# A decoder layer on one core: bfloat16 conversions moved to GpSimd, and the cross attention's output normalization moved from ScalarE into the weights and the residual

## The chip, the cores and the metric

The kernel runs on one core of a Trainium2 chip. The metric is the device time of one execution in microseconds (us). Three runs of the kernel before took 2183.72, 2186.22 and 2188.77 us, so the median is 2186.22 us.

The engines are named as in the profile: PE is TensorE (matrix products and transposes), DVE is VectorE, ACT is ScalarE, POOL is GpSimd, SP is SyncE, which here only issues DMAs. PEld is the loading of weights into TensorE.

## The reference, cut to what matters

The layer takes 32 sequences of 256 tokens with 256 features. It has three parts, each with a residual and a layer norm without gain behind it:

```
x = layernorm(x + self_attention(x))            # 16 heads of 64, 4 key heads, rotary, alibi
x = layernorm(x + cross_attention(x, ctx))      # 16 heads of 16, windows of 64, a mask
x = layernorm(x + ffn(x))                       # 8-bit quantized inputs, ternary weights
```

Two places matter. The cross attention ends in a projection of a normalized row o, with a gain g, a shift b, weights W and a bias:

```
m   = mean(o);  var = mean((o - m)**2)
out = ((o - m) * rsqrt(var + eps) * g + b) @ W.T + bias
```

The feed-forward part quantizes the inputs of its products, once before the gate and up products (256 features) and once before the down product (1024 features):

```
scale = 127 / max(abs(x));  xq = round(x * scale) / scale
```

## The kernel before, in words

All 32 sequences are worked through one after the other, with neighbours overlapped: the self attention of a sequence runs beside the cross attention of the one before and the feed-forward part of the one before that. A sequence has 16 slots (four units m of four parts each). The loop at the end of `tile_decoder_kernel` walks over the slots and emits, by hand, what PE, DVE and ACT do, in that order. Stages that do not belong to the attention's inner units are generators (`self_output`, `cross_inputs`, `cross_output`, `feed_forward`, `prepare_cross`); `yield n` means that the generator goes on n slots later. `last` is a list of operations that `flush()` emits at the end of a part, so an operation put there lands behind the exponentials of that part on ACT.

`tc.manual_schedule` covers PE, DVE and ACT, whose instructions stand in the order of emission. The order on POOL and on SP is set by the framework's planner from what it expects to be ready; in the trace, for example, L186 of the context's normalization runs behind L584, and L184 and L185 run ahead of it. Each engine works through its own queue in order and waits at semaphores for the others.

The lines that the change and the prediction touch:

- `prepare_cross` (from L208) runs once at the start. It multiplies the weights of the four cross projections by the gain of their layer norm (POOL, L224), and the shift through the weights gives a bias (PE, L245; DVE, L252).
- `stats` (L177, L178) computes mean and variance of a row on DVE. `rstd_of` (L184 to L186) makes the factor 1/sqrt(var + eps) and the shift -mean * factor on POOL, in three small instructions. `scaled` (L198) applies both on ACT. `transposed` (L204, L205) transposes a tile on PE and copies it out of PSUM on ACT.
- `cross_output` (from L762) is called for the two halves t of a sequence. It normalizes the row `on` with `stats`, `rstd_of` and `scaled`, transposes it into `zoT`, multiplies it with the weights `xo_w` (PE, L775), adds the residual x1 (DVE, L779), and normalizes the result, x2.
- `feed_forward` (from L786) finds the largest absolute value of x2 on DVE, scales and rounds on POOL by adding MAGIC = 12582912 (L803, output `tr`, in the code xi), takes MAGIC away again with an output in bfloat16 on DVE (L805, `xib`), and lets SP issue transposing DMAs into `xiT` (L809). PE multiplies it with the gate and up weights (L816), ACT takes the tanh (L830), DVE the products (L831, L837). The hidden row `gu` is then treated in the same way: the maximum (L843), four small DVE instructions (L845 to L850), POOL (L852), DVE (L855, `hib`), SP (L857, `hiT`), and the down product on PE (L863).
- Beside them on POOL: the rotary additions (L354, L584 to L586), the copy `R` of the reciprocals of the softmax sums (L455), the mask (L612, L615), and the factors of the other layer norms. `R` waits for a transposing DMA (`planes`) of what DVE spread out in `wide` (L443).
- The attention's own chain: scores on PE (`s`, L393), the maximum and the bias on DVE (`p`, `nm`, L409), exponentials on ACT (L427), transposes on PE (`t`, L471), the copy `pT` on ACT (L480), the products with the values on PE (`o`, L492). The cross attention has the same chain: `xs` (L674), L688, L704, `xt` (L713), the copy `xpT` (L715), `xo` (L729). The context is normalized in `cross_inputs` (`cs` by L198) and transposed into `zcT`. `self_output` makes the normalized row `row` on DVE (L538), transposed into `zqT`, and the query projection `xq` (L550).

Of the kernel before, what the change touches and what calls it, by code (L numbers as in the profile page):

```python
# [10 lines left out]
BF16 = mybir.dt.bfloat16  # L11
# [3 lines left out]
ALU = mybir.AluOpType  # L15
# [36 lines left out]
def kernel(  # L52
# [50 lines left out]
    def work(name, shape, bufs=2, dtype=F32):  # L103
        return sb.tile(list(shape), dtype, tag=name, name=name, bufs=bufs)
# [103 lines left out]
    def prepare_cross():  # L208


        nc.sync.dma_start(vecs_sb, vecs)
        nc.sync.dma_start(cols_sb, cols)
        for j, (w, dst) in enumerate(
            (
                (wxk, xkv_w[:, :, 0:D]),
                (wxv, xkv_w[:, :, D : 2 * D]),
                (wxq, xq_w),
                (wxo, xo_w),
            )
        ):  # L220
            raw = work("tr", [P, NDC, D], 3)
            nc.sync.dma_start(raw, w.rearrange("(c p) n -> p c n", p=P))
            for dc in range(NDC):
                nc.gpsimd.tensor_scalar(  # L224
                    dst[:, dc, :], raw[:, dc, :], vecs_sb[:, j, 0, dc : dc + 1], None, ALU.mult
                )
            if j == 0:
                nc.sync.dma_start(wo_sb, Wo.rearrange("(c p) n -> p c n", p=P))
            if j in xbias:
                more = work("xp", [P, 512])  # L230
                row = more[:, 0:D]
                nc.sync.dma_start(row, rows[j].partition_broadcast(P))
                for dc in range(NDC):
                    nc.gpsimd.tensor_scalar(
                        more[:, D + dc * P : D + (dc + 1) * P],
                        ones,
                        vecs_sb[:, j, 1, dc : dc + 1],
                        None,
                        ALU.mult,
                    )  # L240
            yield 2
            pb = bank("mm")
            if j in xbias:
                for dc in range(NDC):
                    nc.tensor.matmul(  # L245
                        pb[:, 0:D],
                        more[:, D + dc * P : D + (dc + 1) * P],
                        raw[:, dc, :],
                        start=(dc == 0),
                        stop=(dc == NDC - 1),  # L250
                    )
                nc.vector.tensor_tensor(xbias[j], pb[:, 0:D], row, ALU.add)  # L252
            else:
                for ch in range(NDC):
                    for dc in range(NDC):
                        nc.tensor.matmul(
                            pb[:, ch : ch + 1],
                            raw[:, dc, ch * P : (ch + 1) * P],
                            vecs_sb[:, j, 1, dc : dc + 1],
                            start=(dc == 0),  # L260
                            stop=(dc == NDC - 1),
                        )
                nc.vector.tensor_tensor(xbcol[j], pb[:, 0:NDC], cols_sb[:, j, :], ALU.add)
            yield 2
# [497 lines left out]
    def cross_output(b, t):  # L762
        s = state[b]
        on = s["on", t]
        mv = stats(on, "zo")
        rstd = rstd_of(mv, "zo")
        yield
        last.append(partial(scaled, on, on, rstd))
        yield 2
        zoT = work("zT", [P, NDC, P])  # L770
        transposed(zoT, on, "zoT")
        yield 2
        py = bank("xw")
        for dc in range(NDC):
            nc.tensor.matmul(py[:, 0:D], zoT[:, dc, :], xo_w[:, dc, :], start=(dc == 0), stop=(dc == NDC - 1))  # L775
        if t == 0:
            s["x2"] = work("x2", [P, NT, D])
        h = s["x2"][:, t, :]
        nc.vector.tensor_tensor(h, py[:, 0:D], s["x1", t], ALU.add)  # L779
        mv = stats(h, "x2")  # L780
        rstd = rstd_of(mv, "x2")
        yield
        last.append(partial(scaled, h, h, rstd))


    def feed_forward(b):  # L786
        x2 = state[b]["x2"]

        s = small("ffs", NT)
        nc.vector.tensor_reduce(s, x2, AX.X, ALU.max, apply_absolute_value=True)  # L790
        nc.vector.tensor_scalar(s, s, QUANT_MIN, None, ALU.max)
        up = small("ffup", NT)
        nc.vector.reciprocal(up, s)
        nc.vector.tensor_scalar(up, up, 127.0, None, ALU.mult)
        g_of = small("ffg", NT)
        nc.vector.tensor_scalar(g_of, s, ff_scale["gate"], 0.5, ALU.mult, ALU.mult)
        u_of = small("ffu", NT)
        nc.vector.tensor_scalar(u_of, s, ff_scale["up"], None, ALU.mult)
        nc.vector.tensor_tensor(u_of, u_of, g_of, ALU.mult)
        xi = work("tr", [P, NT, D], 3)  # L800
        xib = work("xib", [P, NT, D], 1, BF16)
        for t in range(NT):
            nc.gpsimd.tensor_scalar(xi[:, t, :], x2[:, t, :], up[:, t : t + 1], MAGIC, ALU.mult, ALU.add)  # L803
        yield
        nc.vector.tensor_scalar(xib, xi, MAGIC, None, ALU.subtract)  # L805

        xiT = work("xiT", [P, NT, NDC, P], 1, BF16)
        for t in range(NT):
            nc.sync.dma_start_transpose(xiT[:, t, :, :], xib[:, t, :])  # L809
        yield 3  # L810
        gu = work("gu", [P, NT, INNER], 1)

        def hidden(name, t, half):
            pg = bank("ff")
            for dc in range(NDC):
                nc.tensor.matmul(  # L816
                    pg,
                    xiT[:, t, dc, :],
                    ff_w[name][:, dc, half * 512 : (half + 1) * 512],
                    start=(dc == 0),  # L820
                    stop=(dc == NDC - 1),
                )
            return pg


        for t in range(NT):
            for half in range(2):
                pg = hidden("gate", t, half)
                cols = gu[:, t, half * 512 : (half + 1) * 512]
                nc.scalar.activation(cols, pg, AF.Tanh, scale=g_of[:, t : t + 1])  # L830
                nc.vector.scalar_tensor_tensor(cols, cols, 1.0, pg, ALU.add, ALU.mult)  # L831
            yield 1 if t == 0 else 3
        for t in range(NT):
            for half in range(2):
                pg = hidden("up", t, half)
                cols = gu[:, t, half * 512 : (half + 1) * 512]
                nc.vector.tensor_tensor(cols, cols, pg, ALU.mult)  # L837
            yield 1 + t
        d_ofs, hiTs = [], []
        for t in range(NT):  # L840

            m = small("ffm", 1)
            nc.vector.tensor_reduce(m, gu[:, t, :], AX.X, ALU.max, apply_absolute_value=True)  # L843
            sh = small("ffsh", 1)
            nc.vector.tensor_scalar(sh, m, u_of[:, t : t + 1], QUANT_MIN, ALU.mult, ALU.max)  # L845
            hup = small("ffhup", 1)
            nc.vector.reciprocal(hup, sh)
            nc.vector.tensor_scalar(hup, hup, u_of[:, t : t + 1], 127.0, ALU.mult, ALU.mult)
            d_of = small("ffd", 1)
            nc.vector.tensor_scalar(d_of, sh, ff_scale["down"], None, ALU.mult)  # L850
            d_ofs.append(d_of)
            nc.gpsimd.tensor_scalar(gu[:, t, :], gu[:, t, :], hup, MAGIC, ALU.mult, ALU.add)  # L852
            yield
            hib = work("hib", [P, INNER], 2, BF16)
            nc.vector.tensor_scalar(hib, gu[:, t, :], MAGIC, None, ALU.subtract)  # L855
            hiT = work("hiT", [P, NIC, P], 2, BF16)
            nc.sync.dma_start_transpose(hiT, hib)  # L857
            hiTs.append(hiT)
        yield 2
        for t in range(NT):  # L860
            py = bank("ffo")
            for ic in range(NIC):
                nc.tensor.matmul(  # L863
                    py[:, 0:D], hiTs[t][:, ic, :], ff_w["down"][:, ic, :], start=(ic == 0), stop=(ic == NIC - 1)
                )
            y = x2[:, t, :]
            nc.vector.scalar_tensor_tensor(y, py[:, 0:D], d_ofs[t], y, ALU.mult, ALU.add)
            mv = stats(y, "y")
            rstd = rstd_of(mv, "y")
            yield  # L870
            last.append(partial(scaled, y, y, rstd))
        last.append(partial(nc.sync.dma_start, out[b].rearrange("(t p) d -> p t d", p=P), x2))
        del state[b]
# [179 lines left out]
```

## Time and profile before

| what | value |
|---|---|
| runs, median of three | 2186.22 us (2183.72 to 2188.77) |
| profiled execution, span from first to last instruction | 2184.1 us; no other time of that execution is recorded |
| PE busy | 2096.9 us, 96% |
| DVE busy | 1778.0 us, 81% |
| ACT busy | 1600.0 us, 73% |
| POOL busy | 1285.1 us, 59% |
| mean clock granted to TensorE | 0.983 |
| one 64.65 us stretch from 1015.00 us on: PE, DVE, ACT, POOL busy | 64.21, 55.40, 49.91, 39.88 us |
| HBM traffic | 39.50 MB read, 8.39 MB written |

The profile is one execution on the chip. A row of the groups gives line, engine and operation, output and inputs by name, shapes and count; then the busy time in us and the mean duration in ns; then the idle time of that engine just ahead of these instructions and whose end released them. A row of the waits gives who waited for whom, with the total in us, how often, and the longest. The chain follows the work that ended last back from the end, and gives for each piece its start and its length. Matrix products are pipelined and their ends are modelled, so PE may stand still for some tenths of a microsecond while it counts as busy; such a stall shows when a block of products takes longer than the same block elsewhere. A line can be that of a helper, so L198 or L204 stands for several callers, which the names of the tiles tell apart.

### The profile page before, as it was taken

The page shows a single profiled execution, that of the slowest core. Times are in us where ns is not written, and L with a number is a line of the kernel's source. Part 1 is how long each engine was busy: PE and PEld are TensorE (multiplying, and loading weights), DVE is VectorE, ACT ScalarE, POOL GpSimd, SP SyncE. Part 2 cuts the span into 40 slices and gives each one's busy share as a digit, 9 for nine tenths or more (in the row PEclk, how much of TensorE's full clock was granted, in tenths as well). Part 3 has the DMA queues.
Part 4 walks back from the last instruction along what each step waited for, and adds up shares of the span by engine and source line. Part 5 has one row for each costly group of instructions (what it writes and reads, how often), then busy time and mean ns, then how long its engine had stood idle before and what let it go on. Part 6 is the DMA issues. An engine that isn't in the chain of part 4 may idle for free.

```text
span 2184.1 us, 54367 instructions
## 1 busy us (share of the span) xinstructions
PE 2096.9 (96%) x17316; PEld 1606.7 (74%) x17316; DVE 1778.0 (81%) x6949; ACT 1600.0 (73%) x4833; POOL 1285.1 (59%) x1977
## 2 busy tenths in 40 slices
PE   7899999999999999999999999999999999999983
PEld 5677777777777777777777777777777777777751
DVE  4777888888888888888888888888888888888765
ACT  2478778777778877777877777877777877777862
POOL 4555665566655656655656655656666566666542
PEclk9899999999999999999999999999999999999986
DMA  7432333333333334334334333333343333333211
GB/s 219 111 75 72 82 75 83 77 79 86 89 72 78 83 71 91 86 71 86 76 76 89 82 77 79 78 81 83 86 82 76 81 82 74 90 81 69 53 42 32
DMA packets 326589, 177.57 MB, mean 81 GB/s; under 512 B 242976, under 2 KB 296096, under 8 KB 326304
## 3 DMA queue, kind: packets, MB, share of 16 engines
q1 hardware_dynamic: 324608, 170.52, 34.6%
q8 instruction: 139, 2.28, 0.5%
q10 hardware_dynamic: 1696, 3.57, 0.5%
q14 instruction: 146, 1.20, 0.2%
HBM read 39.50 MB, written 8.39 MB: 22 GB/s over the span
## 4 chain that ended last, share of the span: by engine, by line
PE 74%; DVE 11%; ACT 5%; POOL 4%; DMA 4%; issue 1%; SPq 0%; ACTq 0%; POOLq 0%; DVEq 0%
PE wo L513 10%; PE o L492 8%; PE proj L330 8%; PE t L471 8%; PE s L393 8%; PE ff L816 5%; PE xt L713 4%; PE xo L729 3%; PE xq L550 3%; PE xs L674 3%; PE ffo L863 3%; PE xk L622 3%; DVE p L409 2%; PE xw L775 2%; PE v L362 2%; DVE xib L805 2%
## 5 line engine op out<-in xcount | busy, mean ns | idle before, releaser
L427 ACT ACTIVATE p<-p,nm 128x256 f32<-128x256 f32 x1024 | 511.6, 512 | 197.7 <-DVE nm L409 197.7
L409 DVE CUSTOM_DVE_ANT_0 p<-s,alibi 128x256 f32<-128x256 f32 x1024 | 364.6, 416 | 6.3 <-PE s L393 6.3
L480 ACT COPY pT<-t 128x512 f32<-128x512 f32 x512 | 276.1, 601 | 89.6 <-PE t L471 89.3
L704 ACT ACTIVATE xp<-xp,xnm 128x128 f32<-128x128 f32 x1024 | 331.8, 416 | 0.0
L688 DVE CUSTOM_DVE_ANT_0 xp<-xs,mask 128x128 f32<-128x128 f32 x1024 | 225.9, 285 | 68.1 <-PE xs L674 68.1
L455 POOL COPY R<-planes 128x1024 uint16<-128x1024 uint16 x128 | 175.4, 1370 | 176.3 <-DMA planes<-wide 164.6
L471 PE MATMUL t<-ident,p 128*128 128x128 f32 x2048 | 266.4, 273 | 0.9 <-ACT p L427 0.9
L492 PE MATMUL o<-pT,v 128*64 128x256 f32 x2048 | 260.8, 386 | 1.3 <-ACT pT L480 1.1
L393 PE MATMUL s<-kT,qT 64*128 64x256 f32 x2048 | 255.7, 389 | 0.0
L513 PE MATMUL wo<-wo_sb,oT 128*128 128x256 f32 x1024 | 248.0, 386 | 0.4 <-ACT xpT L715 0.3
L354 POOL TENSOR_TENSOR qT<-qT,other 128x512 f32<-128x512 f32 x128 | 169.4, 1323 | 127.6 <-DMA other<-psin 66.4
L330 PE MATMUL proj<-xT,wq_sb 128*128 128x256 f32 x1024 | 243.1, 381 | 0.0
L471 PEld LDWEIGHTS t<-ident,p 128*128 128x128 f32 x2048 | 234.2, 141 | 9.4 <-ACT p L427 2.6
L393 PEld LDWEIGHTS s<-kT,qT 64*128 64x128 f32 x2048 | 187.3, 186 | 63.4 <-issue 14.3
L492 PEld LDWEIGHTS o<-pT,v 128*64 128x64 f32 x2048 | 143.9, 136 | 104.4 <-issue 21.2
L513 PEld LDWEIGHTS wo<-wo_sb,oT 128*128 128x128 f32 x1024 | 194.9, 193 | 30.9 <-ACT xpT L715 1.1
L427 ACT ACTIVATION_READ_ACCUMULATOR p<-p,nm 128x1 f32 x1024 | 208.0, 203 | 0.0
L330 PEld LDWEIGHTS proj<-xT,wq_sb 128*128 128x128 f32 x1024 | 185.8, 191 | 21.1 <-issue 0.4
L831 DVE SCALAR_TENSOR_TENSOR gu<-gu,ff 128x512 f32<-128x512 f32 x128 | 82.6, 684 | 84.5 <-ACT gu L830 84.3
L713 PEld LDWEIGHTS xt<-ident,xp 128*128 128x128 f32 x1024 | 110.6, 141 | 53.7 <-issue 38.5
L713 PE MATMUL xt<-ident,xp 128*128 128x128 f32 x1024 | 143.3, 281 | 2.1 <-ACT xp L704 2.0
L339 DVE TENSOR_TENSOR psin<-proj,rs_sb 128x512 f32<-128x512 f32 x160 | 109.8, 686 | 38.2 <-PE proj L330 34.6
(146 smaller groups left out, 4325.7 us busy)
## 6 DMA issues: line engine op xcount, KB each, us to landing
other<-psin SPq DMA_DIRECT2D x640, 64.0 KB, 2.0
xT<-in_xt_dram SPq DMA_DIRECT2D x32, 256.0 KB, 2.8
xs<-in_x_dram SPq DMA_DIRECT2D x32, 256.0 KB, 2.8
cs<-in_ctx_dram SPq DMA_DIRECT2D x32, 256.0 KB, 2.8
other<-qb SPq DMA_DIRECT2D x64, 128.0 KB, 2.1
kTz<-tr SPq DMA_DIRECT2D x256, 32.0 KB, 2.0
other<-qb SPq DMA_DIRECT2D x128, 64.0 KB, 2.0
out_dram<-x SPq DMA_DIRECT2D x32, 256.0 KB, 2.3
```

The lines of the kernel that those rows point to most:

```text
L330: nc.tensor.matmul(pq[:, c * L : (c + 1) * L], w[:, dc, c * P : (c + 1) * P], xT[:, dc, :], start=(dc == 0), stop=(dc == NDC - 1),)
L393: nc.tensor.matmul(banks[half][:, rr * L : (rr + 1) * L], qT[rows_, rr, qc * P : (qc + 1) * P], kT[rows_, kc, :], start=(rr == 0), stop=(r ...
L409: nc.vector.tensor_tensor_reduce(p[:, cols], banks[half][:, cols], alibi[:, 2 * (4 * kc + 2 * rp + rr) + half, :], -0.125, 3.0e38, ALU.add ...
L427: nc.scalar.activation(p[:, cols], p[:, cols], AF.Exp, bias=nm[:, rr : rr + 1], scale=-1.0, accum_out=s["sums", i // 2][:, e : e + 1],)
L455: nc.gpsimd.tensor_copy(R.bitcast(U16).rearrange("p (n z) -> p z n", z=2), s.pop(("planes", m)).rearrange("p z r q -> p z (r q)"),)
L471: nc.tensor.transpose(pt[:, j * P : (j + 1) * P], p[half][:, rr * L + kk * P : rr * L + (kk + 1) * P], ident,)
L480: nc.scalar.copy(pT, pt)
L492: nc.tensor.matmul(po[half * HD : (half + 1) * HD, rp * L : (rp + 1) * L], s["v"][:, kk, (2 * kc + half) * HD : (2 * kc + half + 1) * HD], ...
L513: nc.tensor.matmul(py[:, 0:D], s["oT", qc, kc][:, r, :], wo_sb[:, 4 * kc + r, :], start=(kc == 0 and r == 0), stop=(kc == 1 and r == 3),)
L688: nc.vector.tensor_tensor_reduce(p[:, cols], banks[2 * half + j // 2][:, j % 2 * P : (j % 2 + 1) * P], s["mask"][:, qc, :], -1.0, 3.0e38, ...
L704: nc.scalar.activation(p[:, cols], p[:, cols], AF.Exp, bias=s["xnm", i][half][:, j : j + 1], scale=-1.0)
L713: nc.tensor.transpose(pt[:, j * P : (j + 1) * P], p[:, j * P : (j + 1) * P], ident)
```

## The change

There are three edits. First, `prepare_cross` centres the weights of the cross output once: a product with ones gives the sum over the input features, and 1/D of it is subtracted from each row of weights. A row multiplied by such weights loses its mean by itself. Second, `cross_output` no longer normalizes `on` in front of the transpose: `rstd_of`'s third instruction and the ACT operation are gone, the transpose takes `on` as it is, in the same slot as before, and the factor is applied to the projection in the instruction that adds the residual. Third, the two conversions to bfloat16, `xib` and `hib`, are done by POOL in place of DVE, straight behind the POOL instructions that make their inputs and one yield earlier in the order of emission; `xib` in two instructions, one for each half.

```diff
@@ prepare_cross
                 nc.vector.tensor_tensor(xbias[j], pb[:, 0:D], row, ALU.add)
+                if j == O_:
+                    for dc in range(NDC):
+                        nc.tensor.matmul(pb[:, D:], ones, dst[:, dc, :], start=(dc == 0), stop=(dc == NDC - 1))
+                    for dc in range(NDC):
+                        nc.vector.scalar_tensor_tensor(
+                            dst[:, dc, :], pb[:, D:], -1.0 / D, dst[:, dc, :], ALU.mult, ALU.add
+                        )
@@ cross_output
         mv = stats(on, "zo")
-        rstd = rstd_of(mv, "zo")
-        yield
-        last.append(partial(scaled, on, on, rstd))
-        yield 2
+        rstd = small("rstd_zo", 1)
+        nc.gpsimd.tensor_scalar(rstd, mv[:, 1:2], EPS, None, ALU.add)
+        nc.gpsimd.tensor_tensor(rstd, rstd, neg_half[:, 0:1], ALU.pow)
+        yield 3
         zoT = work("zT", [P, NDC, P])
...
-        nc.vector.tensor_tensor(h, py[:, 0:D], s["x1", t], ALU.add)
+        nc.vector.scalar_tensor_tensor(h, py[:, 0:D], rstd, s["x1", t], ALU.mult, ALU.add)
@@ feed_forward
             nc.gpsimd.tensor_scalar(xi[:, t, :], x2[:, t, :], up[:, t : t + 1], MAGIC, ALU.mult, ALU.add)
+        for t in range(NT):
+            nc.gpsimd.tensor_scalar(xib[:, t, :], xi[:, t, :], MAGIC, None, ALU.subtract)
         yield
-        nc.vector.tensor_scalar(xib, xi, MAGIC, None, ALU.subtract)
...
             nc.gpsimd.tensor_scalar(gu[:, t, :], gu[:, t, :], hup, MAGIC, ALU.mult, ALU.add)
+            hib = work("hib", [P, INNER], 2, BF16)
+            nc.gpsimd.tensor_scalar(hib, gu[:, t, :], MAGIC, None, ALU.subtract)
             yield
-            hib = work("hib", [P, INNER], 2, BF16)
-            nc.vector.tensor_scalar(hib, gu[:, t, :], MAGIC, None, ALU.subtract)
             hiT = work("hiT", [P, NIC, P], 2, BF16)
             nc.sync.dma_start_transpose(hiT, hib)
```

## The prediction

> **What bounds the kernel now.** I read four views of the profile, in this order: the busy shares, the waits, the chain that ended last, and the groups of instructions. The shares say that TensorE (PE) is the engine to look at:
>
> ```profile
> PE 2096.9 (96%) x17316; PEld 1606.7 (74%) x17316; DVE 1778.0 (81%) x6949; ACT 1600.0 (73%) x4833; POOL 1285.1 (59%) x1977
> ```
>
> One sequence repeats every 64.65 us (a 64.65 us stretch from 1015 us on has PE busy for 64.21 us at a granted clock of 1.00). So a gain can only come from PE's few stalls, and from the two ends of the span. The waits name those stalls; the columns are total us, times, longest:
>
> ```profile
> PE xo L729 <- ACT xpT L715: 12.0, 30, 0.7
> ...
> PEld o L492 <- ACT pT L480: 8.2, 33, 1.5
> ...
> PE zqT L204 <- DVE row L538: 6.7, 10, 1.7
> ```
>
> The first two come about once for each of the 32 sequences; the third is irregular. The chain around the first (start us, length us, what) shows its origin:
>
> ```profile
> 1041.62 1.46 DVE xib L805
> ...
> 1046.53 0.59 ACT x L539
> 1047.11 0.98 ACT p L427 x4
> 1048.10 0.96 ACT xpT L715 x2
> 1049.06 0.04 issue
> 1049.10 0.43 PE xo L729 x16
> ...
> 1056.46 2.33 PE o L492 x16
> ```
>
> VectorE's bfloat16 conversion xib sits ahead of the softmax pieces p. They come late, ScalarE's exponentials start late, and from 1044.05 to 1063 us ScalarE has no idle time in its timeline. PE pays twice. First at xo: from the start of xs (1047.54) to the start of xq (1049.46) are 1.92 us, against 0.62 + 0.59 = 1.21 us for the same two blocks at 1029.71 and 1062.98: 0.71 us. Then at o, 2.33 us against 1.88 us at 1021.15: 0.45 us. Together 1.16 us in each sequence.
>
> Why does xib take 1.46 us? The groups:
>
> ```profile
> L855 DVE TENSOR_SCALAR hib<-gu 128x1024 bf16<-128x1024 f32 x64 | 58.1, 908 | 8.9 <-POOL gu L852 8.9
> L805 DVE TENSOR_SCALAR xib<-tr 128x512 bf16<-128x512 f32 x32 | 44.3, 1384 | 8.3 <-POOL tr L803 7.5
> L852 POOL TENSOR_SCALAR gu<-gu,ffhup 128x1024 f32<-128x1024 f32 x64 | 71.7, 1120 | 79.2 <-DVE ffhup L848 79.0
> L803 POOL TENSOR_SCALAR tr<-x,ffup 128x256 f32<-128x256 f32 x64 | 29.9, 480 | 0.0
> ```
>
> The fastest xib took 426 ns, the median 1482 ns. At 1041.54 to 1042.81 POOL runs L585, and xib, issued at 1041.60, ends 0.28 us after it. This DVE form stands still while POOL works.
>
> **The change part by part.**
>
> *xib leaves DVE.* 1.48 us go from the stretch in front of p. On DVE: the statistics of on, then p from about 1042.2 instead of 1043.56; the scores exist by then (PE issued that unit's half from 1040.76 to 1041.7). ScalarE starts at about 1042.7 instead of 1044.05. Its order then is four exponentials (1.97 us), two scalings (1.0), two exponentials (1.0), the two copies xpT (0.95): done at 1047.6, and PE wants them at 1048.16. The stall of 0.71 goes, with some 0.5 us to spare. What is late next is L538, a conversion-free DVE TENSOR_SCALAR that can be held up by POOL too (409 ns usual, 1259 ns when it fell on L586); even held until 1045.0 it leaves these copies in time.
>
> *on's scaling leaves ScalarE.* 64 ACTIVATE of 599 ns, some 0.5 us of it in each place because neighbours overlap. One lies at 1050.20, between the two stalls. PE comes to o 0.71 us earlier, so o's second copy has to be earlier by more than that. The activation gu L830 after it needs PE's gate product, which bounds its start to about 1050.3 instead of 1051.46; the copy ends 1.16 us earlier, at 1056.05, where PE would want it at 1055.95. I take 0.34 of the 0.45 us. Sum of both stalls: 0.71 + 0.34 = 1.05 us a sequence, 29 times: **-30.5 us**.
>
> *The factor at the residual.* L779 becomes a scalar_tensor_tensor; L867 is that form (476 against 422 ns): 64 x 0.054 = 3.5 us of DVE, hidden as DVE idles 45.2 us ahead of L779 for PE. Its new wait on POOL's rstd costs nothing: at 1045.55 the factor is there, L779 runs at 1060.71. Were POOL 15 us late, the p pieces behind L779 would wait, and ScalarE for them. POOL loses L186, 64 x 265 ns = 17 us.
>
> *The centring*, once: four matmul records (0.86 us after the 0.43 us records of L245) and two DVE instructions of about 0.48 us in front of the first scores at 35.3 us, where PE waits for DVE and ScalarE afterwards. Nothing at best (2.6 us of waiting at 58.5 us can hide it), 1.8 us at worst; I take +0.9.
>
> *hib and xib on POOL.* No row shows POOL subtracting one constant with a bfloat16 output. Lower end: the two-operation multiply and add at 1120 ns for 1024 columns and 480 for 256, so 0.83 ns a column and 0.27 fixed. Upper end: L612, a compare and a multiply, 721 ns for 128 columns, so 3.5 ns a column and 3.9 us for a hib. Between them lie the only one-operation rows:
>
> ```profile
> L224 POOL TENSOR_SCALAR xkv_w<-tr,vecs_sb 128x256 f32<-128x256 f32 x4 | 3.7, 932 | 12.0 <-DMA tr<-in_wxk_dram 11.6 <-DMA tr<-in_wxv_dram 0.3
> L234 POOL TENSOR_SCALAR xp<-ones,vecs_sb 128x128 f32<-128x128 f32 x4 | 2.4, 604 | 0.0
> ```
>
> Their medians are 924 and 602 ns: (0.924 - 0.602) / 128 = 2.52 ns a column, 0.28 fixed. They have the second operation left out, as the new instructions have, so I take them: **hib 2.86 us, xib 2 x 0.92 us**. POOL grows by 64 x 2.86 + 64 x 0.92 - 17 = 225 us, from 59 to 69%.
>
> The Trainium skill speaks both ways here. Its "GPSIMD Engine Reference", section 4.1, calls one-input work on this engine roughly line-rate, which would put a hib near 1.16 us (an estimate from the page's 1.03 cycles at 1.2 GHz, section 3.1, and the same fixed part) and the whole change at the second case below; L224's 932 ns for 256 columns does not agree. Its "SBUF — State Buffer", section "SBUF: two separate sides", says that a GpSimd instruction and a VectorE one in a two-port mode exclude each other for a whole instruction; the 1.48 us of xib agrees, and by that rule longer POOL instructions hold up what DVE still has of the kind.
>
> *What waits behind them.* xib: POOL's L585, L586, the rstd, a qT addition and L540 move 1.85 us later, into 2.80 us in which POOL waits ahead of the mask L612: hidden. hib of t = 0 starts at 1014.1, into 3.5 us of idle, and would hold up the DVE copy wide (L443, 694 ns; 1678 ns once when POOL was on) by about 1.0 us; hib's own 0.6 us of DVE is gone, so DVE is 0.4 us late. hib of t = 1 stands ahead of the copy R and of the normalization of the context (L184 to L186), on which ScalarE's cs and PE's zcT wait. In twelve sequences from 572 us on I put gu's end + 2.95 us in the place of R's start and followed to cs: the context's factors move by 1.7 to 3.0 us, most was slack, and zcT is late by 0 to 1.5 us, 0.6 us on average. x29: **+17 us**. On SP the transposing DMA hiT of t = 1 is issued about 2 us later, and four issues of L312 behind it; the qT addition they feed comes after the same POOL work anyway.
>
> *Ends of the span.* In the last two sequences nothing hides POOL. From the end of hup at 2140.39 to the end of the second hib are 5.6 us; with POOL doing gu, hib, gu, hib it is 2 x (1.12 + 2.86) + 0.23 = 8.2: +2.6, twice, and +0.5 for xib: +5.7. Against it about -2.5 around 2045 to 2093, where xib's 1.49 and on's 0.49 stand in the chain. **+3.2.**
>
> **Sum**: -30.5 + 0.9 + 17 + 3.2 = -9 on the execution's span of 2184.1: 2175. The median of the runs, 2186.2, lies 2.1 above that span, and I carry this over: **2177 us**.
>
> **The rivals.**
>
> *POOL at its fast price* (1.12 us for a hib, as L852). Then R and the context's factors hardly move (0.07 us), zcT has over 1 us of slack, and at the end 2 x 2.24 + 0.23 = 4.7 is 0.9 shorter than 5.6, twice. -30.5 + 0.9 - 1.8 - 2.5 = -34: 2150 of span, 2152 us. For it: the same opcode; against: L224.
>
> *POOL becomes the late engine*, slower than before. The place is hib of t = 1 ahead of the context's factors. At L612's price, 3.9 us, zcT waits 0.6 + 1.0 = 1.6 us: 29 x (1.6 - 1.05) = +16, the ends +9.3 - 2.5, the centring +0.9: 2208 of span, 2210 us. With zcT's wait at 0.6 + (h - 2.86) the change breaks even at h of about 3.15 us, only 0.3 above my price. The same would follow if the planner put more work behind hib.
>
> *Nothing moves*: with both stalls relieved another late copy of ScalarE stops PE a few blocks on, since ScalarE runs without a gap there: 2184 to 2188 us.
>
> **How the numbers follow.** Forecast 0.52, fast POOL 0.24, late POOL 0.17, nothing 0.07. 0.2% is 4.4 us, about what a measurement of this kernel can tell from no change. The forecast's own spread (zcT's wait 0.3 to 1.0 us) is 2168 to 2189: 0.35 faster, 0.10 same, 0.07 slower. With fast POOL (0.24 faster), late POOL (0.17 slower) and nothing (0.05 same, 0.01 faster, 0.01 slower): faster 0.60, same 0.15, slower 0.25. The range reaches from the fast case to most of the late one: 2149 to 2205.
>
> **What would show it.** The group of hib on POOL: 2.8 us or 1.1. PE's wait xo on xpT gone, and PE o back at 1.88 us. PE's wait zcT on cs new, in under half of the sequences beyond 0.5 us. DVE's copy wide near 1.7 us. In the end, 8.2 us from hup to the second hib. Wrong would be: xpT still late (xib wasn't the origin), or a new PE wait that no step here names.

## The result, and the profile after

The changed kernel takes 2274.26 us (median of four runs, 2266.82 to 2278.43), against 2187.07 us for the kernel before on the same chip: ratio 1.0399, interval [1.038, 1.0418]. It is about 4% slower, and lies 69 us over the end of the predicted range. The profiled execution of it has a span of 2270.4 us (before: 2184.1) and a mean granted clock of 0.967 (before: 0.983).

The busy shares come first, on the page of the changed kernel. Line numbers are 7 higher than before from the end of `prepare_cross` on, and 8 higher from xiT's transposes on.

```profile
PE 2141.6 (94%) x17258; PEld 1639.8 (72%) x17320; DVE 1752.7 (77%) x6855; ACT 1583.5 (70%) x4769; POOL 1487.1 (66%) x2041
```

Two things are to be seen. POOL's 202 us more is about the 225 us that were foreseen. But PE is busy for 45 us more although it multiplies no more than before (but for four records at the start), so its instructions have become longer: that is the clock, further down. (In kernel 1 below, which has no halved clock in the middle of the span, PE is busy for 2092.6 us.)

The groups of POOL show the price of the conversions (mean ns last ahead of the idle time):

```profile
L862 POOL TENSOR_SCALAR hib<-gu 128x1024 bf16<-128x1024 f32 x64 | 178.4, 2788 | 5.2
...
L812 POOL TENSOR_SCALAR xib<-tr 128x256 bf16<-128x256 f32 x64 | 54.6, 868 | 0.0
```

The prediction took 2.86 and 0.92 us; 2.79 and 0.87 are the values. So the loss is not a mispriced instruction. The waits of PE (total us, times, longest), first one row of before, then after:

```profile
PE xs L674 <- POOL xqT L586: 4.4, 3, 3.6
```

```profile
PE xs L681 <- POOL xqT L593: 19.9, 24, 5.0
PE wo L520 <- ACT xpT L722: 16.1, 28, 1.0
PE xs L681 <- DMA kTz<-tr: 16.0, 30, 0.7
...
PE zcT L204 <- ACT cs L198: 3.4, 2, 2.4
```

The wait of xo on xpT (12.0 us in 30 times) is down to 1.0 us in two, as foreseen. Of the rows after, the second belongs to the context's chain that the prediction named, though at wo and not at zcT. The first has grown from 4.4 us in three places, the third from 0.2 us in one, and no step of the prediction has them: PE waits at xs for the cross attention's queries xqT and keys kTz, the keys in nearly every sequence. That is one of the prediction's own signs of being wrong, a new PE wait that no step names.

Who makes kTz late? Its DMAs are issued by SP. The same view for SP, first before, then after:

```profile
SPq L312 <- DVE kT L346: 299.2, 30, 11.4
...
SPq L809 <- DVE nm L409: 28.8, 26, 1.4
```

```profile
SPq L319 <- DVE kT L353: 290.4, 29, 10.1
SPq L817 <- POOL xib L812: 223.0, 31, 7.6
```

L817 issues xiT's transposes. Before, SP waited there for 1.1 us at a time, and the profile names xib in three of these waits (3.1 us together); after, it stands for xib, 7.2 us in each sequence. SP's timeline of one sequence tells why (start, length, what). Before, with the product xv starting at 1038.94:

```profile
1034.85 1.16 SPq L573 DMA_DIRECT2D other<-qb  x2
1039.90 2.47 SPq L312 DMA_DIRECT2D other<-psin  x4
...
1043.74 2.49 SPq L809 DMA_TRANSPOSE xiT<-xib  x2
...
1055.94 4.70 SPq L658 DMA_DIRECT2D kTz<-tr  x7
```

After, with xv at 1071.54:

```profile
1067.83 1.16 SPq L580 DMA_DIRECT2D other<-qb  x2
1075.66 2.46 SPq L817 DMA_TRANSPOSE xiT<-xib  x2
1078.21 2.46 SPq L319 DMA_DIRECT2D other<-psin  x4
1080.77 0.54 SPq L656 DMA_DIRECT2D xvaug<-xvaug  x1
1081.41 0.54 SPq L657 DMA_DIRECT2D xvaug<-xvaug  x1
...
1089.35 0.58 SPq L580 DMA_DIRECT2D other<-qb  x1
1089.98 4.69 SPq L665 DMA_DIRECT2D kTz<-tr  x7
```

The order is another one. The planner, which sets SP's queue, has moved xiT's transposes ahead of the four issues of psin and the two of xvaug. They wait for xib, and everything behind them waits too. From there on SP issues without a gap. The last issue of kTz ends 23.13 us after the start of xv in place of 21.70. The last issue of other<-qb, an input of the queries, is late in the same way: on average over 22 sequences it starts 17.64 us behind the start of xv in place of 15.45, and xqT ends at 23.00 in place of 21.04.

PE's timeline at the end of that sequence:

```profile
1094.81 0.90 PE L681 MATMUL xs<-kTz,xqT 32*128 32x256 f32 x6 [0.66 <-POOL xqT L593]
1096.22 0.67 PE L681 MATMUL xs<-kTz,xqT 32*128 32x256 f32 x2 [0.51 <-DMA kTz<-tr]
1096.81 0.65 PE L736 MATMUL xo<-xpT,xvaug 128*32 128x64 f32 x32
```

PE waits 0.66 us for xqT, and then from xs to xo are 2.00 us, where an undisturbed block takes 0.62: the last key is late. A second loss follows at such places. Busy time in three windows around the next one; the value after the engines is the granted clock of PE:

```profile
1160.00:1166.00 6.00, 5.34 (x54) 3.86 (x55) 3.90 (x25) 3.92 (x15) 2.73 (x4) 0.97 0.26 56
1166.00:1169.40 3.40, 3.18 (x22) 2.08 (x14) 2.23 (x6) 0.97 (x2) 1.63 (x4) 0.54 0.40 77
1169.40:1200.00 30.60, 30.19 (x245) 23.39 (x247) 24.55 (x91) 22.89 (x71) 21.43 (x29) 1.00 0.37 73
```

Right behind the stall the clock is halved for 3.41 us. From 110 to 2060 us there are 19 such places, 68.3 us together; before there is none. What they cost shows in the sequences: from xo to the next xv are 43.07 us in the 19 sequences that have such a place, and 41.28 us in the seven others whose xv starts between 230 and 1990 us. That is 1.8 us each, 34 us in all.

### The profile page after: what moved, and what is told of

Same layout as the page of the kernel before. It is cut to its first block, busy times and chain, and to the rows that moved or that the text cites. A ratio compares the mean times of both kernels' runs of the same rounds, so it can differ in the third digit from the quotient of the medians.

```text
span 2270.4 us, 54276 instructions
## 1 busy us (share of the span) xinstructions
PE 2141.6 (94%) x17258; PEld 1639.8 (72%) x17320; DVE 1752.7 (77%) x6855; ACT 1583.5 (70%) x4769; POOL 1487.1 (66%) x2041
## 4 chain that ended last, share of the span: by engine, by line
PE 75%; DVE 7%; DMA 5%; POOL 4%; ACT 4%; SPq 3%; issue 3%; POOLq 0%; DVEq 0%; ACTq 0%
PE o L499 9%; PE s L400 9%; PE wo L520 9%; PE proj L337 9%; PE t L478 8%; PE xt L720 5%; PE ff L824 4%; PE xs L681 4%; PE xo L736 3%; DMA kTz<-tr 3%; PE xk L629 2%; PE xv L641 2%; PE xq L557 2%; SPq L665 2%; PE v L369 2%
## 5 line engine op out<-in xcount | busy, mean ns | idle before, releaser
L520 PE MATMUL wo<-wo_sb,oT 128*128 128x256 f32 x1024 | 261.8, 401 | 16.1 <-ACT xpT L722 16.1
L520 PEld LDWEIGHTS wo<-wo_sb,oT 128*128 128x128 f32 x1024 | 206.2, 204 | 59.7 <-ACT xpT L722 22.8
L862 POOL TENSOR_SCALAR hib<-gu 128x1024 bf16<-128x1024 f32 x64 | 178.4, 2788 | 5.2
L681 PE MATMUL xs<-kTz,xqT 32*64 32x256 f32 (+1 forms) x1536 | 120.0, 411 | 37.9 <-POOL xqT L593 19.9
```

What stands on the lines that cost most here:

```text
L520: nc.tensor.matmul(py[:, 0:D], s["oT", qc, kc][:, r, :], wo_sb[:, 4 * kc + r, :], start=(kc == 0 and r == 0), stop=(kc == 1 and r == 3),)
L681: nc.tensor.matmul(banks[r][:, 0 : 2 * P].rearrange("p (h k) -> p h k", k=P)[q0:q1], s["xqT", qc][rows_, ch, q0:q1], kTz[rows_, ch, :, k0 ...
```

## The experiments

All ratios are against the kernel before on the same chip. "Behind xv" in this text means measured from the start of the product xv, mean of 22 sequences, in the profiled execution.

### 1: SP's order as before, all else as changed

```diff
-            nc.sync.dma_start_transpose(xiT[:, t, :, :], xib[:, t, :])
+            tc.keep_in_program_order(nc.sync.dma_start_transpose(xiT[:, t, :, :], xib[:, t, :]))
```

> The changed kernel, with one thing altered: the two transposing DMAs xiT are pinned in SP's queue to their place in the order of emission, behind the four issues of psin's turn (other<-psin) and the two of xvaug, where they stand in the kernel before. In the changed kernel the planner put them ahead of these. Theory 1 (SP's order: the head of SP's queue waits some 6 us for POOL's xib, all later issues slip, kTz lands late, PE waits at xs and its clock is then halved for a while): the xs wait (about 2.2 us a sequence) and the half-clock stretches go, zcT's wait stays: about 2190 us, 2175 to 2205. Theory 2 (POOL itself is late, its rotations and xqT come too late for xs whatever SP does): hardly anything changes, 2245 or more.

Measured: 2193.81 us, ratio 1.0045 [1.003, 1.006], span 2194.1. Theory 1. No stretch at half clock is left in the middle of the span, xs to xo takes 0.72 us. SP's place for xiT is worth 76.3 us of span. POOL's instructions are as long as in the changed kernel (hib 2787 ns, xib 866), and yet xqT ends at 20.91 us behind xv: POOL's length is not what made the queries late. The waits of PE now:

```profile
PE wo L520 <- ACT xpT L722: 22.1, 28, 1.0
...
PE zcT L204 <- ACT cs L198: 8.7, 11, 2.4
PE xs L681 <- POOL xqT L593: 6.0, 3, 3.1
```

What remains is the wait at wo. Its origin, in one sequence of this kernel, on POOL:

```profile
1020.26 2.79 POOL L862 TENSOR_SCALAR hib<-gu 128x1024 bf16<-128x1024 f32 x1
1023.02 0.57 POOL L185 TENSOR_TENSOR rstd_zc<-rstd_zc,neg_half 128x1 f32<-128x1 f32 x1
...
1023.83 1.34 POOL L462 COPY R<-planes 128x1024 uint16<-128x1024 uint16 x1
1025.26 0.26 POOL L186 TENSOR_SCALAR rstd_zc<-mv_zc,rstd_zc 128x1 f32<-128x1 f32 x1
```

then on ACT:

```profile
1025.56 0.60 ACT L198 ACTIVATE cs<-cs,rstd_zc 128x256 f32<-128x256 f32 x1 [1.57 <-POOL rstd_zc L186]
1027.02 0.60 ACT L198 ACTIVATE cs<-cs,rstd_zc 128x256 f32<-128x256 f32 x1 [0.86 <-POOL rstd_zc L186]
...
1028.51 1.04 ACT L722 COPY xpT<-xt 128x512 f32<-128x512 f32 x2
```

and on PE:

```profile
1027.67 0.44 PE L204 MATMUL zcT<-ident,cs 128*128 128x128 f32 x2 [0.44 <-ACT cs L198]
1029.13 1.99 PE L520 MATMUL wo<-wo_sb,oT 128*128 128x256 f32 x8 [1.02 <-ACT xpT L722]
```

hib, and the copy R that follows it, hold up the context's factors, ACT stands at cs for 1.57 and 0.86 us, and behind cs in ACT's queue are two exponentials and the copies xpT, which wo waits for by the profile's releaser. PE pays 0.44 and then 1.02 us.

### 2 and 3: one conversion at a time back on DVE

Kernel 2 (xib on DVE, hib on POOL) and kernel 3 (hib on DVE, xib on POOL), SP's order left to the planner:

```diff
-        for t in range(NT):
-            nc.gpsimd.tensor_scalar(xib[:, t, :], xi[:, t, :], MAGIC, None, ALU.subtract)
         yield
+        nc.vector.tensor_scalar(xib, xi, MAGIC, None, ALU.subtract)
```

```diff
-            nc.gpsimd.tensor_scalar(hib, gu[:, t, :], MAGIC, None, ALU.subtract)
             yield
+            nc.vector.tensor_scalar(hib, gu[:, t, :], MAGIC, None, ALU.subtract)
```

> The changed kernel with xib back on DVE in its old place; hib stays on POOL. SP's order of xiT is then that of the kernel before. Theory 1: no xs wait; the stall of 0.7 us at xo comes back, zcT's wait stays: about 2205 us, 2190 to 2220. Theory 2 (POOL's load, of which hib is 178 us of the 233 added): still 2240 or more.

Measured: 2227.6 us, ratio 1.0198 [1.0181, 1.0215], span 2227.0. It is 8 us over the range. SP's order is the old one here (psin at 1.16 us behind xv, xiT at 5.30). The stall at xo is back, and the one at wo is there:

```profile
PE wo L520 <- ACT xpT L722: 20.8, 28, 1.0
PE xo L736 <- ACT xpT L722: 13.1, 31, 0.7
```

> The changed kernel with hib back on DVE in its old place; xib stays on POOL, and with it the planner's place of xiT at the head of SP's queue. Theory 1: the xs wait stays and zcT's wait goes: about 2245 us, 2225 to 2262. Theory 2: most of POOL's added load is gone, so most of the loss is: 2195 or less.

Measured: 2209.58 us, ratio 1.0126 [1.0097, 1.0155], span 2208.9. It falls between the ranges of both theories. xiT stands ahead of psin here, so moving xib alone brings the new order. xs to xo takes 2.17 us, and six places show half clock, 23.9 us. The wait at wo is down to 0.2 us in one place.

### 4: the kernel before, with psin behind xiT on SP

The four issues of psin of one slot are held back until the part's other stages have run, which puts them behind xvaug and xiT:

```diff
-            nc.sync.dma_start(dst[i * half : (i + 1) * half, :], src[j * half : (j + 1) * half, :])
...
+        if slot % 16 == 11:
+            held.append(issue)
...
+                while held:
+                    held.pop(0)()
```

> The kernel before, with both conversions on DVE and the old normalization; only SP's order is altered: the four issues of psin's turn of that slot are emitted and pinned behind the two xiT transposes. POOL's work is that of the kernel before. Theory 1: the issues wait for xib, everything behind them on SP slips by 4 to 6 us, xs waits: 2235 to 2285 us. Theory 2: no change, 2184 to 2195.

Measured: 2185.81 us, ratio 1.0002 [0.9989, 1.0014], span 2179.0. Theory 1 fell: this order by itself costs nothing. psin goes out at 6.86 us behind xv, as late as in the changed kernel (6.56). But the order is not wholly that of the changed kernel. In one sequence, with xv at 1035.11:

```profile
1037.49 0.47 SPq L661 DMA_DIRECT2D xvaug<-xvaug  x1
1038.06 0.55 SPq L662 DMA_DIRECT2D xvaug<-xvaug  x1
1039.31 2.46 SPq L821 DMA_TRANSPOSE xiT<-xib  x2
1041.86 2.45 SPq L314 DMA_DIRECT2D other<-psin  x4
```

xvaug's two issues, 1.3 us with their gaps, go out before xiT, while xib is still on its way; in the changed kernel they stand behind psin. So the last kTz issue ends at 22.05 and not at 23.20. PE, which still has its stall at xo, starts xs at 23.52 and not at 23.07. The table sets the arrival of the last key and the end of the queries xqT beside PE's (us behind xv; from issue to landing kTz takes 2.0 us by the changed kernel's page):

| kernel | last kTz issue ends, plus 2.0 | xqT ends | PE starts xs | xs to xo |
|---|---|---|---|---|
| before | 23.09 | 21.04 | 23.66 | 0.64 |
| 4: before, psin behind xiT | 24.05 | 22.22 | 23.52 | 0.84 |
| changed | 25.20 | 23.00 | 23.07 | 2.30 |
| 1: changed, old SP order | 22.77 | 20.91 | 22.53 | 0.72 |
| 3: hib on DVE | 24.78 | 22.65 | 22.78 | 2.17 |
| 8: two operations, new SP order | 24.46 | 22.37 | 22.59 | 2.02 |

The further PE comes to xs ahead of the last key, the longer the block: half a microsecond ahead costs 0.2 us, two cost 1.4 to 1.7. (In the changed kernel the start of xs already holds 0.48 us of waiting for xqT.) Taking xib off DVE brings PE there 1.1 us earlier (before against 1), and the same step puts xib at the head of SP's queue, which makes the keys 1 to 2 us later. Neither of the two alone was dear: the one is kernel 6 below, the other kernel 4. But kernel 4 has only 1 us of the keys' delay; no run has the whole 2 us with xib on DVE, and by the table these would have stalled PE too, if less.

### 5: the layer norm part alone

Both conversions are on DVE, as in the diffs of 2 and 3 together.

> Only the layer norm part is done: centred weights, factor at the residual; xib and hib are converted by DVE as before the change. Theory 1 (xib's conversion on DVE is what makes the copies xpT late, so the two stalls of PE stay; hib's length on POOL is what cost xib-on-DVE 42 us): about 2183 us, 2176 to 2189; PE's first score block xs and xo stand where they stood before. Theory 2 (the layer norm part bears some of the loss of the run with xib on DVE): 2195 us or more, with a new wait of PE behind the residual L779 or the transposes zoT.

Measured: 2180.02 us, ratio 0.9972 [0.9961, 0.9984], span 2176.6. Theory 1. The layer norm part bears no loss; alone it is worth 5 us.

### 6: hib on DVE, xib on POOL, SP's order as before

The second diff of 2 and 3, with the line of 1.

> The changed kernel with hib's conversion back on DVE and with xiT's transposes held to their place in SP's queue, behind the four psin issues; xib stays on POOL. Theory 1 (the loss is SP's order and hib's length, the gain is xib's leaving DVE, 1.0 us a sequence): about 2154 us, 2146 to 2165; no stretch at half clock. Theory 2 (the 1.1 us that the pinned kernel lost again belongs to no part of the change but to whatever is late next once PE comes 1 us earlier): 2180 to 2195 us.

Measured: 2155.78 us, ratio 0.9855 [0.9839, 0.987], span 2154.7. Theory 1. Two places of half clock are left between 110 and 2060 us. Where hib's length is gone, so are nearly all of both waits: wo on xpT is down to 0.6 us in two places, and ACT's wait at cs between 300 and 2000 us (the last two numbers of its group: idle time ahead, and the part for rstd_zc) falls from kernel 1

```profile
L198 ACT ACTIVATE cs<-cs,rstd_zc 128x256 f32<-128x256 f32 x52 | 31.2, 600 | 70.2 <-POOL rstd_zc L186 70.2
```

to kernel 6

```profile
L198 ACT ACTIVATE cs<-cs,rstd_zc 128x256 f32<-128x256 f32 x54 | 29.3, 590 | 5.1 <-POOL rstd_zc L186 4.3
```

The four kernels before, 5, 6 and 1 make one ladder with the changed one. By spans: layer norm part 2176.6 - 2184.1 = -7.5; xib to POOL 2154.7 - 2176.6 = -21.9; hib to POOL 2194.1 - 2154.7 = +39.4; SP's new order 2270.4 - 2194.1 = +76.3. Together +86.3. The steps are not independent of their order: hib on POOL costs 50.4 with xib still on DVE (5 to 2) and 61.5 with SP's new order (3 to the changed kernel), and SP's new order costs 54.2 with hib on DVE (6 to 3).

### 7 and 8: the conversions as two operations

```diff
-            nc.gpsimd.tensor_scalar(xib[:, t, :], xi[:, t, :], MAGIC, None, ALU.subtract)
+            nc.gpsimd.tensor_scalar(xib[:, t, :], xi[:, t, :], 1.0, -MAGIC, ALU.mult, ALU.add)
...
-            nc.gpsimd.tensor_scalar(hib, gu[:, t, :], MAGIC, None, ALU.subtract)
+            nc.gpsimd.tensor_scalar(hib, gu[:, t, :], 1.0, -MAGIC, ALU.mult, ALU.add)
```

Kernel 7 has the line of 1 as well, kernel 8 leaves SP's order to the planner.

> The pinned kernel with both conversions on POOL written as two operations, times 1.0 and plus -MAGIC, in place of one subtraction; the numbers computed are the same. Theory 1 (one missing second operation makes POOL slow, as L224 against L860): hib about 1.12 us, xib about 0.48 us a half, and the time 2145 to 2160 us, as hib no longer holds up the context's factors. Theory 2 (the bfloat16 output or the constants set POOL's pace): hib stays at 2.8 us and the time at 2190 to 2197 us.

> The changed kernel, SP's order as the change has it (xiT first), with both conversions written as two operations. If POOL then takes 1.12 us for hib and 0.48 for half of xib, xib is ready 0.8 us earlier: by theory 1 (SP's order) about a third of the delay of kTz goes and hib's part all, so 2165 to 2200 us, about 2180, still over the pinned kernel of this pair by 15 us or more. By theory 2 (POOL's length alone made the loss): 2145 to 2160, no more than 6 us from the pinned one.

Measured: 7 takes 2151.09 us, ratio 0.9833 [0.9815, 0.9851], span 2150.7; 8 takes 2188.76 us, ratio 1.0012 [0.9997, 1.0027], span 2186.7. Theory 1 in both. The groups of POOL in 7:

```profile
L862 POOL TENSOR_SCALAR hib<-gu 128x1024 bf16<-128x1024 f32 x64 | 67.0, 1047 | 5.2
...
L812 POOL TENSOR_SCALAR xib<-tr 128x256 bf16<-128x256 f32 x64 | 25.1, 410 | 0.0
```

The same numbers are computed in 38% of the time for hib, in 47% for xib. Even so SP's order costs 36 us of span in 8, since xib is still at its head: xs to xo takes 2.02 us against 0.70 in 7, 1.32 us in some 30 sequences, 40 us. Only two places of half clock show in either, so here the stall by itself accounts for the loss.

### 9: what makes POOL slow

Kernel 1 with hib as two operations in the other order, and xib as one addition:

```diff
-            nc.gpsimd.tensor_scalar(xib[:, t, :], xi[:, t, :], MAGIC, None, ALU.subtract)
+            nc.gpsimd.tensor_scalar(xib[:, t, :], xi[:, t, :], -MAGIC, None, ALU.add)
...
-            nc.gpsimd.tensor_scalar(hib, gu[:, t, :], MAGIC, None, ALU.subtract)
+            nc.gpsimd.tensor_scalar(hib, gu[:, t, :], MAGIC, 1.0, ALU.subtract, ALU.mult)
```

> The pinned kernel with two other forms of the conversions on POOL: hib as two operations, minus MAGIC and then times 1.0; xib as one operation, plus -MAGIC. The numbers computed are the same. Theory 1 (the second operation that is left out makes POOL slow): hib 1.05 us and half of xib 0.87 us; the time as with both in two operations or a little above it, 2150 to 2158 us. Theory 2 (the subtraction makes it slow): hib 2.8 us and half of xib 0.41 us; the time near the pinned kernel's, 2186 to 2196 us.

Measured: 2222.89 us, ratio 1.0184 [1.0161, 1.0207], span 2224.6. The groups of POOL, and two waits of PE:

```profile
L862 POOL TENSOR_SCALAR hib<-gu 128x1024 bf16<-128x1024 f32 x64 | 233.9, 3655 | 5.2
...
L812 POOL TENSOR_SCALAR xib<-tr 128x256 bf16<-128x256 f32 x64 | 55.2, 876 | 0.0
```

```profile
PE wo L520 <- ACT xpT L722: 27.4, 28, 1.0
PE zcT L204 <- ACT cs L198: 17.6, 22, 3.4
```

Neither theory holds. One operation costs the same whether it subtracts or adds (868 and 876 ns), and a second operation does not make it faster: subtract and then multiply takes 3655 ns, 1.31 times one subtraction. Of the forms tried only the pair multiply, add is fast. The run also gives one more point for hib's length, below; its time holds eight places of half clock between 110 and 2060 us, 27.3 us together, where kernel 1 has none.

### 10 and 11: the best versions

Kernel 10 is 6 with xib as multiply and add. Kernel 11 is 7 with the layer norm part undone, so only the conversions differ from the kernel before.

> xib on POOL in two operations, hib on DVE, xiT's transposes held to their place. Theory 1 (once hib on POOL takes 1.05 us it costs no more than on DVE, and xib has slack of more than 0.5 us): 2148 to 2157 us, about 2153, within 4 us of the kernel with both on POOL in two operations. Theory 2 (0.6 us of hib on DVE still stands in PE's way): 2157 us or more.

> Only the conversions: both on POOL in two operations, xiT's transposes held to their place, and cross output's layer norm as before the change (ScalarE scales on, no centring of the weights). Theory 1 (the layer norm part is worth the 5 us of its run alone, the conversions the rest): 2151 plus 5, 2153 to 2162 us. Theory 2 (the layer norm part is what lets PE profit from the earlier xpT, since it takes 0.5 us a sequence half off ScalarE, which makes those copies): 2165 us or more, with a PE wait on xpT back.

Measured: 10 takes 2151.98 us, ratio 0.9856 [0.9834, 0.9879]; 11 takes 2144.23 us, ratio 0.9824 [0.9806, 0.9843], span 2141.5. Kernel 10 is theory 1: hib as multiply and add on POOL is no dearer than on DVE. It also stands where 6 stands (0.9855), so xib's length has slack, as the prediction had it. Kernel 11 is under both ranges. Its interval overlaps that of 7, so with the conversions right nothing can be told of the layer norm part, while the 5 us of kernel 5 do not add up with the rest. Kernels 7 and 11 beat both kernels of the case, the one before by 1.7 and 1.8%.

## Why the prediction was wrong

**The step that failed** is in "What waits behind them". The prediction kept SP's order as the trace of before had it, and followed xib only along POOL ("into 2.80 us in which POOL waits ahead of the mask L612: hidden"). On POOL that is right: with SP's order kept, xqT ends at 20.91 us behind xv (kernel 1), at 21.04 before. But xib's consumer is a DMA in SP's queue, whose order the planner makes anew; it went from behind psin and xvaug to the head, and the queue waited behind it, the keys and the inputs of the queries among the rest. For SP the prediction named hiT alone, and held its delay for harmless.

Kernel 1 puts the price at 76 us. The 26 sequences whose xv starts between 230 and 1990 us, set against those of kernel 1, show where it lies: 0.59 us more until xs starts, for xqT; 1.57 us more from xs to xo, for kTz; 1.8 us of halved clock in 19 of them; and 0.50 us less in the rest, as the waits at wo and zcT have shrunk (16.1 and 3.4 us in place of 22.1 and 8.7). That is 15 + 41 + 34 - 13 = 77 us.

Without this step the prediction would still have had the wrong sign: kernel 1 is 0.4% slower and not 0.4% faster. That is the size of two terms, further down: hib cost 39.4 us of span where +17 and 5.7 at the end were held, and xib's leaving DVE gave 21.9 us where the two stalls were to give 30.5.

**Both stalls go, -30.5.** The one at xo went wholly (0.71 us). Of that at o, 0.34 us were to go. Measured from the start of the block to the start of the next, mean of 22 sequences, it takes 2.26 us before and 2.20 after, against 1.88 elsewhere: 0.06 went. The stall had also been read too large: 2.33 us is the block's length in PE's timeline, where an undisturbed one has 1.95, so it was 0.38 us and not 0.45. xib's leaving DVE gave 21.9 us of span (5 to 6). That the prediction split the o part off for the layer norm part was wrong: in 11, without it, the same block takes 2.11 us.

**zcT, +17.** The mechanism was right, hib ahead of the context's factors; the size was not. Against 0.6 us a sequence, PE's waits at zcT and wo come to 22.1 + 8.7 us in kernel 1, of which some 4 us are in 6 too: 27 us, 0.9 each. The prediction followed cs to zcT, but not what stands behind cs on ACT, the copies xpT. In all hib costs 39.4 us of span (6 to 1): 32.0 between the first xv and the last, 6.1 behind the last, and 1.3 ahead of the first.

**The ends, +3.2.** From the last xv to the end of the span are 111.4 us before and 114.6 after: right, and so are its parts. Kernel 6, without hib's part, has 109.1, kernel 1 has 115.2: -2.3 and +6.1 against -2.5 and +5.7. (The two pieces named for the -2.5, 1.49 and 0.49 us, add up to 2.0 only.) From hup to the second hib are 8.03 us, 8.2 foreseen.

**The centring, +0.9**: the first scores start at 37.6 us in place of 35.2. Kernels without it have 34.8 to 36.5, those with it 36.2 to 38.4, on average 35.5 and 37.3. So it is nearer to the 1.8 us that were given as the worst case, in ranges that overlap.

**POOL's price, 2.86 us**: right, and the rows of one operation were the ones to take. That the missing second operation is what makes them slow, as experiment 7 had it, kernel 9 refutes. The upper end of 3.9 us was misread: 721 ns is L612's form on 64 partitions, its form on 128 takes 1239 ns.

**The fast POOL rival, 2152 us**, named what kernel 7 shows, 2151.09: a hib of 1.05 us, hardly a wait at zcT, the stall at xo gone. It needs SP's old order too; without it (8) there is no gain.

**The late POOL rival, 2210 us**, named the right place, with the point from which it decides too high. With SP's order kept, a hib of 1.05, 2.79 and 3.66 us gives ratios of 0.9833, 1.0045 and 1.0184 (kernels 7, 1 and 9). (xib's length differs too, but 6 and 10 show that it doesn't matter.) Part of the last is half clock, which the other two hardly have. The line between the first two crosses 1 at 1.05 + 1.74 x 0.0167 / 0.0212 = 2.4 us, not at 3.15. So by this rival alone, at the price that was forecast, the change would have been slower by 0.4%.

**"Nothing moves"** falls: 6 and 7 turn the relieved stall into time.

What stays open: the cost of the halved clock is a comparison of sequences, no run took it away alone; the changed kernel's whole order on SP was not run with xib on DVE; why kernel 5 gains 5 us was not located, nor why hib costs more with xib on DVE (kernel 2, 8 us over its range); and why the planner moved xiT was not looked into beyond this, that 3 and 8 have the move and 2 does not.

## What to carry to other kernels

Where a planner orders a queue, moving a producer can reorder its consumers: before a step is called hidden, look at the queue that issues the DMA behind it, and ask what happens if that DMA is the first in line. A relieved stall brings the bounding engine earlier to its next input, and that input's slack (here 0.6 us) has to be priced with the gain. When an engine's instruction must move to GpSimd, compare forms that compute the same numbers before choosing the engine.

## What the runs showed of the hardware

**POOL's tensor_scalar depends on the pair of operations.** For 1024 columns with bfloat16 output: multiply, add 1047 ns; one subtraction 2788; subtract, multiply 3655. The Trainium skill, "GPSIMD Engine Reference", section 4.1, calls one-input work roughly line-rate; the multiply and add agrees with it (1.16 us by the estimate in the prediction), the other two forms do not.

**The clock is halved behind stalls much shorter than one stretch of its record.** In the changed kernel I cut the time from 110 to 2060 us into 571 stretches of 3.41 us, as the clock's record has them. PE stood idle for 0.8 us or more in 23 of them; 17 of these were followed by a stretch at half clock, and 3 of the 548 others. But idle time as recorded does not decide: in kernel 1 there are 14 stretches with 0.8 to 1.48 us, and none was followed. The record hides the lengthening of the block xs. With it (idle time ahead of xs, plus what xs to xo takes over 0.62 us) the stall at xs was 1.7 us or more in 43 sequences of the changed kernel, 3 and 8 together, and 27 of these had a halved clock behind it; of the 43 with a shorter stall none had. In kernel 9, whose halved places but one lie elsewhere, all seven stretches with 1.67 us of idle time or more were followed, and none of the 20 with 0.8 to 1.45 us. The Trainium skill, "TensorE: Matmul & The Clock Gate", section "HAM oscillation", gives as the abstract rule no idle gaps over about 3.4 us; here stalls of 1.7 us, half of that, were enough in most places.

**How long DVE's copy wide takes beside a GpSimd instruction goes by that instruction's form, not by its length.** The mean of all copies is 709 ns before and 1015 in the changed kernel. In the changed kernel, in kernel 1 and in kernel 9 alike, 29 copies start while a hib runs, on average 1.80 us after its start. Beside a hib of one subtraction (2.79 us) they took 1480 and 1474 ns, and ended 0.49 us after the hib. Beside the longer hib of kernel 9 (subtract, multiply, 3.66 us) they took 703, and ended while it still ran. The prediction had 1.7 us, from the length of POOL's instructions. Why the forms differ was not looked into.
